# A state-space recurrence with its states in the partitions, sums by TensorE, and three smaller edits

## The chip, the cores and the metric

The kernel runs on one core of a Trainium2 chip. The metric is the device time of one execution in microseconds (us), as the median of several runs. One execution was also recorded by the hardware profiler; the line numbers (L1053) are those of the kernel before. PE is TensorE, DVE VectorE, ACT ScalarE, POOL GpSimd; SP issues DMAs.

## The reference

Six layers run one after the other over x of 64 sequences x 32 steps x 256 channels, each added to x: cross-attention to a context of 257 rows (stage 0), a time-mixing layer with a recurrence (1), a mixture of experts with the two best of eight (2), a quantized cross-attention (3), a state-space layer (4) and a mixture of eight experts (5). The change touches stages 0, 4 and 5. Cut to what matters, stage 0 is

```python
q = querys @ Wq.T + bq
k = keys @ Wk.T + bk
v = values @ Wv.T + bv
scores = jnp.einsum('bnd,bmd->bnm', q, k)
```

and stage 4, with 512 inner channels d and 16 states n, is

```python
ssm = xc @ x_proj_w.T + x_proj_b
B_param = ssm[..., :d_state]
C_param = ssm[..., d_state:2 * d_state]
delta = jax.nn.softplus(ssm[..., -1:])
A = -jnp.exp(A_log)
def step(h, ts):
    dt, B_t, C_t, x_t = ts
    dA = jnp.exp(A[None] * dt[:, :, None])
    dBx = dt[:, :, None] * B_t[:, None, :] * x_t[:, :, None]
    h = dA * h + dBx
    y = jnp.einsum('bdn,bn->bd', h, C_t) + D * x_t
    return (h, y)
```

followed by `y * silu(z)`, an output projection with a bias, the residual and a layer norm. Stage 5 begins with `logits = xf @ gate_w.T + gate_b`.

## The kernel before

The 2048 rows of x stay in SBUF as four blocks of 512 (16 sequences of 32 steps). The stages are written block by block in `layers`, in an order that lets one block's stage 4 run beside the next block's stage 3: `gates`, `ahead` of the next block, `recur`, stage 3 of the block after that, stage 5 of the block before. A scheduler takes each engine's instructions from that text and orders them, so that instructions of several stages alternate in each engine's queue; each queue is then worked through strictly in that order. Buffers come from pools with a fixed number of copies per tag, and whoever wants a copy waits until its last reader is done. Nearly all transfers of size are issued by SP, in one queue.

Stage 0. `head` (L173) normalizes a block, brings it to channels in partitions (`xnT`), makes q from it with Wq (L189, bias on ACT at L190), then `qk` from q with Wk (L196), so that scores are `qk` against the raw context (L241), with `qb` (L202) for the bias of the keys. `attend` ends with the value projection (L280) and its bias, a matmul of one row of ones against `bv` (L281).

Stage 4. `ahead` (L968) normalizes, projects (L965), convolves (L990), and makes `ssm` of 32 rows, B and C (L1000), which go to DRAM (`rows`, L1004). The step is made by a second product, with a weight column repeated 128 times, so that it stands in all partitions (`dt_ps`, L1008); a softplus of ACT and DVE instructions (L1013 to L1022) makes `dt`. All these PSUM tiles come from the pool `psp`, which has one buffer; so do those of `gates` (L1030), which makes `silu(z)`.

`recur` (L1032) has 128 of the 512 channels in the partitions and (sequence, step) along the free dimension. `dtx` = dt times the input is made by one POOL instruction (L1036). For each of 16 states, B's and C's rows are broadcast to all partitions (`bc`, L1045, 512 KB, two buffers); for each pair of channel groups POOL makes `g` = dtx times B (L1048), ACT makes the decay `h` = exp(A dt) into PSUM (L1052, two buffers), DVE runs the scan over it (L1053) and multiplies with C (`hc`, L1054), and POOL adds `hc` to `y` (L1055), which ACT had scaled with D (L1041). Then `y` is multiplied with the gate (L1058), projected (L1065), given its bias by a matmul of one row (L1066), added and normalized.

Stage 5. `block` makes gate logits with a bias by a matmul of one row (L1117), then 32 groups of up projections (L1160), gelu on ACT (L1164) and down projections (L1168), with PSUM tiles from `psu`, one buffer; w1 and w2 are loaded per expert by SP (L1155, L1156).

Of the kernel before, what the change touches and what calls it, by code (L numbers as in the profile page):

```python
# [135 lines left out]
def _stage0(k, pool):  # L136
# [11 lines left out]
    wq = _load_w(k, w, "L0_xattn_WqT", 2, D)  # L148
    wkk = _load_w(k, w, "L0_xattn_Wk", 2, D)
    wv = _load_w(k, w, "L0_xattn_WvT", 2, D)  # L150
    bv = w.tile([1, D], F32, name="bv", tag="bv")
    nc.scalar.dma_start(bv, i["L0_xattn_bv"])
# [3 lines left out]
    nc.vector.tensor_scalar(off, off, 0.0, None, ALU.is_equal)  # L156
    neg = w.tile([P, S], F32, name="neg", tag="neg")
# [15 lines left out]
    def head(b):  # L173
        x = k.x[b]
        xs = [x[:, j, :] for j in range(4)]
        mv, rstd = _stats(k, xs, "0", sm0)
        xn = blk.tile([P, 4, D], F32, name="xn", tag="xn")
        for j in range(4):
            _norm(k, xn[:, j, :], xs[j], mv, rstd, j)
        xnT = blk.tile([P, 2, BT], F32, name="xnT", tag="xT", bufs=3)  # L180
        _to_channels(
            k, [xn[:, j, :] for j in range(4)], lambda c, ps: nc.scalar.copy(xnT[:, c, :], ps),
            lambda shape, name: pa.tile(shape, F32, name=name, tag="a"),
        )
        qT = blk.tile([P, 2, BT], F32, name="qT", tag="xT", bufs=3)
        for o in range(2):
            ps = pa.tile([P, BT], F32, name="qps", tag="a")
            for c in range(2):
                nc.tensor.matmul(ps, wq[:, c, o * P : (o + 1) * P], xnT[:, c, :], start=c == 0, stop=c == 1)  # L189
            nc.scalar.activation(qT[:, o, :], ps, AF.Identity, bias=_chan(k, "L0_xattn_bq", o))  # L190

        qk = blk.tile([P, 2, BT], F32, name="qk", tag="xT", bufs=3)
        for d in range(2):
            ps = pa.tile([P, BT], F32, name="qkps", tag="a")
            for o in range(2):
                nc.tensor.matmul(ps, wkk[:, o, d * P : (d + 1) * P], qT[:, o, :], start=o == 0, stop=o == 1)  # L196
            nc.scalar.copy(qk[:, d, :], ps)
        qb = sm0.tile([P, 4], F32, name="qb", tag="qb")
        ps = pb.tile([P, 4], F32, name="qbps", tag="b")
        for j in range(4):  # L200
            for o in range(2):
                nc.tensor.matmul(  # L202
                    ps[:, j : j + 1], qT[:, o, j * P : (j + 1) * P], _chan(k, "L0_xattn_bk", o),
                    start=o == 0, stop=o == 1,
                )
        nc.scalar.copy(qb, ps)
        return qk, qb
# [28 lines left out]
    def attend(b, j, qk, qb, cT, cn, cl):  # L236
# [42 lines left out]
        for c in range(2):  # L279
            nc.tensor.matmul(o_ps, avT[:, c, :], wv[:, c, :], start=c == 0, stop=False)  # L280
        nc.tensor.matmul(o_ps, k.ones[0:1, :], bv, start=False, stop=True)  # L281
# [636 lines left out]
def _stage4(k, w, wk):  # L918
# [3 lines left out]

    nc, i = k.nc, k.i
# [4 lines left out]
    bx = w.tile([2 * N, 1], F32, name="bx", tag="bx")  # L928
    nc.scalar.dma_start(bx, i["L1_attn_x_proj_b"][0 : 2 * N, :])
    bdt = w.tile([P, 1], F32, name="bdt", tag="bdt")  # L930
    nc.scalar.dma_start(bdt, i["L1_attn_x_proj_b"][2 * N, :].partition_broadcast(P))
    rows = w.tile([40, D], F32, name="brows", tag="brows")
    bout, k.b2 = rows[0:1, :], rows[32:40, :]
    nc.scalar.dma_start(bout, i["L1_attn_out_proj_b"])
# [5 lines left out]
    A = w.tile([P, C, N], F32, name="A", tag="A")  # L940
    nc.scalar.dma_start(A, i["L1_attn_A_log"].rearrange("(c p) n -> p c n", p=P))
# [3 lines left out]

    wdt = w.tile([P, C, P], F32, name="wdt", tag="wdt")
    nc.vector.tensor_copy(wdt, wx[:, :, 2 * N : 2 * N + 1].to_broadcast([P, C, P]))
# [8 lines left out]
    def pp(shape, name):  # L956
        return k.psp.tile(shape, F32, name=name, tag="p")
# [10 lines left out]
    def ahead(b):  # L968
# [9 lines left out]
        _to_channels(k, xn, lambda c, ps: nc.scalar.copy(v.xT[:, c, :], ps), pp)  # L978

        xc = wk.tile([P, C, 16, T], F32, name="xc", tag="xc")  # L980
        for c in range(C):
            xpad = xpads[c % 2]
            nc.scalar.activation(
                xpad[:, :, 3:], project(v, c, pp).rearrange("p (b t) -> p b t", t=T), AF.Identity, bias=_chan(k, "L1_attn_in_proj_b", c)
# [11 lines left out]


        ssm_ps = pp([2 * N, BT], "ssm_ps")
        for c in range(C):
            nc.tensor.matmul(ssm_ps, wx[:, c, 0 : 2 * N], v.y[:, c, :], start=c == 0, stop=c == C - 1)  # L1000
        ssm = tmp([2 * N, BT], "ssm")
        nc.scalar.activation(ssm, ssm_ps, AF.Identity, bias=bx)
        v.rows = k.dram.tile([2 * N, BT], F32, name="rows", tag="rows", bufs=2)
        nc.sync.dma_start(v.rows, ssm)  # L1004

        dt_ps = pp([P, BT], "dt_ps")
        for c in range(C):
            nc.tensor.matmul(dt_ps, wdt[:, c, :], v.y[:, c, :], start=c == 0, stop=c == C - 1)  # L1008


        dt = v.dt = wk.tile([P, BT], F32, name="dt", tag="dt")
        e_, u_, l_ = (tmp([P, BT], n) for n in ("e_", "u_", "l_"))
        nc.scalar.activation(dt, dt_ps, AF.Identity, bias=bdt)  # L1013
        nc.scalar.activation(e_, dt_ps, AF.Abs, bias=bdt)
# [8 lines left out]

        return v

    def gates(v):

        v.zs = wk.tile([P, C, BT], F32, name="zs", tag="zs", bufs=1)
        for c in range(C):
            nc.scalar.activation(v.zs[:, c, :], project(v, C + c, pp), AF.Silu, bias=_chan(k, "L1_attn_in_proj_b", C + c))  # L1030

    def recur(b, v):  # L1032
        xs = [k.x[b][:, j, :] for j in range(4)]
        dt, y = v.dt, v.y
        dtx = wk.tile([P, C, BT], F32, name="dtx", tag="dtx", bufs=1)
        nc.gpsimd.tensor_tensor(dtx, y, dt.unsqueeze(1).to_broadcast([P, C, BT]), ALU.mult)  # L1036

        nc.gpsimd.memset(dt.rearrange("p (b t) -> p b t", t=T)[:, :, 0:1], 1e20)

        for c in range(C):  # L1040
            nc.scalar.activation(y[:, c, :], y[:, c, :], AF.Copy, scale=_chan(k, "L1_attn_D", c))  # L1041
        bc_rows = v.rows.rearrange("(two n) t -> n two t", two=2)
        for n in range(N):
            bc = wk.tile([P, 2, BT], F32, name="bc", tag="bc", bufs=2)
            nc.sync.dma_start(bc, bc_rows[n].partition_broadcast(P))  # L1045
            for c2 in range(0, C, 2):
                g = wk.tile([P, 2, BT], F32, name="g", tag="g", bufs=2)
                nc.gpsimd.tensor_tensor(g, dtx[:, c2 : c2 + 2], bc[:, 0:1, :].to_broadcast([P, 2, BT]), ALU.mult)  # L1048
                hc = wk.tile([P, 2, BT], F32, name="hc", tag="hc", bufs=2)
                for c in range(2):  # L1050
                    h = ph([P, BT], "h")
                    nc.scalar.activation(h, dt, AF.Exp, scale=A[:, c2 + c, n : n + 1])  # L1052
                    nc.vector.tensor_tensor_scan(h, h, g[:, c, :], 0.0, ALU.mult, ALU.add)  # L1053
                    nc.vector.tensor_tensor(hc[:, c, :], h, bc[:, 1, :], ALU.mult)  # L1054
                nc.gpsimd.tensor_tensor(y[:, c2 : c2 + 2], y[:, c2 : c2 + 2], hc, ALU.add)  # L1055

        for c2 in range(0, C, 2):
            nc.gpsimd.tensor_tensor(y[:, c2 : c2 + 2], y[:, c2 : c2 + 2], v.zs[:, c2 : c2 + 2], ALU.mult)  # L1058
        xn = wk.tile([P, 4, D], F32, name="xe4", tag="hc", bufs=2)
        xn = [xn[:, j, :] for j in range(4)]  # L1060
        for j in range(4):
            _norm(k, xn[j], xs[j], v.mv, v.rstd, j)
            ps = ph([P, D], "outps")
            for c in range(C):
                nc.tensor.matmul(ps, y[:, c, j * P : (j + 1) * P], wout[:, c, :], start=c == 0, stop=False)  # L1065
            nc.tensor.matmul(ps, k.ones[0:1, :], bout, start=False, stop=True)  # L1066
            nc.vector.tensor_tensor(xn[j], ps, xn[j], ALU.add)
# [13 lines left out]
def _stage5(k, w, out):  # L1081
# [5 lines left out]
    bg = w.tile([1, E], F32, name="bg", tag="bg")  # L1087
    nc.scalar.dma_start(bg, i["L1_ffn_gate_b"])
# [9 lines left out]
    for o in range(2):  # L1098
        nc.tensor.matmul(bs_ps[:, o : o + 1], k.b2[:, o * P : (o + 1) * P], k.ones[32 : 32 + E, 0:1], start=True, stop=True)
# [3 lines left out]
    def block(b):  # L1103
# [12 lines left out]
        for j in range(4):  # L1116
            nc.tensor.matmul(lg_ps[:, j, :], k.ones[0:1, :], bg, start=True, stop=False)  # L1117
            for c in range(2):
                nc.tensor.matmul(lg_ps[:, j, :], xT[:, c, j * P : (j + 1) * P], wg[:, c, :], start=False, stop=c == 1)  # L1119
# [9 lines left out]
        nc.vector.tensor_copy(lg, lg_ps)  # L1129
# [144 lines left out]
def _layouts(inputs):  # L1274
# [11 lines left out]
        "L0_xattn_WqT": a["L0_xattn_Wq"].T,  # L1286
        "L0_xattn_Wk": a["L0_xattn_Wk"],
        "L0_xattn_WvT": a["L0_xattn_Wv"].T,
        "L0_xattn_bv": a["L0_xattn_bv"][None, :],
# [7 lines left out]
    for n in ("L1_xattn_ln_gamma", "L1_xattn_ln_beta", "L1_attn_ln_gamma", "L1_attn_ln_beta", "L1_attn_A_log"):  # L1297
        o[n] = a[n]
    for n in ("in_proj", "x_proj", "out_proj"):
        o[f"L1_attn_{n}T"] = a[f"L1_attn_{n}_w"].T  # L1300
    o["L1_attn_x_proj_b"] = a["L1_attn_x_proj_b"][:, None]
    o["L1_attn_out_proj_b"] = a["L1_attn_out_proj_b"][None, :]
    o["L1_ffn_gate_wT"] = a["L1_ffn_gate_w"].T
    o["L1_ffn_gate_b"] = a["L1_ffn_gate_b"][None, :]
# [24 lines left out]
```

## Time and profile before

| | us |
|---|---|
| median of 3 runs (lowest, highest) | 2099.14 (2093.59, 2099.62) |
| the profiled execution | 2096.84 |
| its span, first to last instruction | 2095.1 |
| recurrence of block 0, 1, 2, 3 (windows from the span's start) | 776 to 1013, 1104 to 1326, 1443 to 1654, 1757 to 1913 |
| stage 5 of the last block | 1951 to 2095 |

The page divides the span into 40 equal slices; each digit is the busy share in tenths:

```profile
PE   4778966669979788656487798887888987787798
...
DVE  5587584775584559889767988655888755876100
ACT  3445342304434174444146566356557445664232
POOL 4445445312121325667625777513767634998000
```

One slice is 52 us. The recurrences lie in slices 16 to 37. A matmul's end is modelled, and passes overlap by their tails, so a busy PE is not a full one; a float32 matmul of the kernel is two passes in the trace. In the lines of groups, the columns are line, engine, operation, output and inputs, count, then busy us, mean ns of one, and after the second bar the engine's idle us just before such instructions, with what ended it.

### The profile page before, as it was taken

What the parts mean: (1) busy time and instruction counts of PE and PEld (TensorE: products, weight loads), DVE (VectorE), ACT (ScalarE), POOL (GpSimd) and SP (SyncE); (2) the same over time, 40 slices, a digit from 0 to 9 for tenths busy, and PEclk for the clock granted to TensorE, in tenths of its full rate; (3) what the DMA queues carried; (4) which work ended last, traced back from release to release, by engine and by line L of the source; (5) the groups of instructions that cost most, each with busy time, mean ns of one, the idle gap of its engine ahead of it and who ended that gap; (6) DMA issues with size and microseconds to landing.
All of it is one profiled execution on the core that took longest, in us unless ns stands there. A gap on an engine that the chain in (4) does not pass through costs nothing. (4 is left out here: it accounts for less than half of the span.)

```text
span 2095.1 us, 20245 instructions
## 1 busy us (share of the span) xinstructions
PE 1644.2 (78%) x6455; PEld 834.1 (40%) x6455; DVE 1391.0 (66%) x2444; ACT 952.6 (45%) x2009; POOL 1013.9 (48%) x1037
## 2 busy tenths in 40 slices
PE   4778966669979788656487798887888987787798
PEld 2334534335545434433234344433444433233343
DVE  5587584775584559889767988655888755876100
ACT  3445342304434174444146566356557445664232
POOL 4445445312121325667625777513767634998000
PEclk8677977889989898558687899888799887999799
DMA  7654232210001011121011232112232112332021
GB/s 239 219 182 144 91 120 80 79 34 21 21 21 43 17 42 51 30 61 61 0 50 53 80 91 90 31 41 65 71 88 73 49 31 66 89 111 77 30 81 40
DMA packets 87540, 149.93 MB, mean 72 GB/s; under 512 B 7672, under 2 KB 51978, under 8 KB 85386
## 3 DMA queue, kind: packets, MB, share of 16 engines
q1 hardware_dynamic: 84868, 147.69, 23.0%
q10 hardware_dynamic: 2566, 0.96, 0.2%
q8 instruction: 51, 0.84, 0.2%
q14 instruction: 55, 0.45, 0.1%
HBM read 137.71 MB, written 10.91 MB: 71 GB/s over the span
## 5 line engine op out<-in xcount | busy, mean ns | idle before, releaser
L1048 POOL TENSOR_TENSOR g<-dtx,bc 128x1024 f32<-128x1024 f32 x128 | 300.4, 2353 | 194.8 <-DVE h L1053 89.4
L1053 DVE TENSOR_TENSOR_SCAN h<-h,g 128x512 f32<-128x512 f32 x256 | 307.3, 1218 | 49.9 <-ACT h L1052 35.1
L1160 PE MATMUL up<-xT,w 128*128 128x512 f32 x512 | 288.1, 678 | 42.5 <-ACT hid L1162 37.3
L1055 POOL TENSOR_TENSOR xc<-xc,hc 128x1024 f32<-128x1024 f32 x128 | 301.0, 2356 | 26.5 <-DVE hc L1054 14.8
L1168 PE MATMUL acc<-hid,w 128*128 128x512 f32 x512 | 250.9, 610 | 15.8 <-ACT hid L1164 15.7
L1052 ACT ACTIVATE h<-dt,A 128x512 f32<-128x512 f32 x256 | 174.0, 692 | 184.5 <-DVE hc L1054 183.3
L1054 DVE TENSOR_TENSOR hc<-h,bc 128x512 f32<-128x512 f32 x256 | 169.7, 679 | 2.9 <-POOL xc L1055 0.5
L1160 PEld LDWEIGHTS up<-xT,w 128*128 128x128 f32 x512 | 97.3, 209 | 165.3 <-issue 79.2
L839 ACT ACTIVATE p<-sc,nm 128x256 f32<-128x256 f32 x256 | 117.6, 471 | 94.5 <-DVE nm L835 83.2
L1162 ACT ACTIVATE hid<-up,chan 128x512 f32<-128x512 f32 x128 | 87.2, 681 | 159.5 <-PE up L1160 159.4
L614 PE MATMUL weps<-we,xT 128*128 128x512 f32 x256 | 139.3, 665 | 17.2 <-DVE x L616 13.9
L1168 PEld LDWEIGHTS acc<-hid,w 128*128 128x128 f32 x512 | 94.1, 194 | 128.2 <-issue 96.3
L828 PE MATMUL sc<-kT,qm 32*128 32x256 f32 x512 | 131.6, 448 | 14.9 <-DVE od L867 11.5
L852 PE MATMUL pt_ps<-ident,p 128*128 128x128 f32 x512 | 97.0, 328 | 53.7 <-ACT p L839 26.6
L833 DVE TENSOR_REDUCE nm<-sc 128x2 f32<-128x512 f32 x128 | 86.3, 686 | 56.2 <-PE sc L828 55.1
L89 POOL TENSOR_TENSOR rs_t<-rs_r 128x4 f32<-128x4 f32 (+3 forms) x138 | 29.7, 218 | 183.1 <-DVE rs_r L87 157.0
L852 PEld LDWEIGHTS pt_ps<-ident,p 128*128 128x128 f32 x512 | 69.5, 165 | 107.1 <-ACT p L839 64.4
L828 PEld LDWEIGHTS sc<-kT,qm 32*128 32x128 f32 x512 | 81.5, 208 | 70.5 <-DVE od L867 20.7
L230 POOL TENSOR_TENSOR cT<-cT,scb 128x2056 f32<-128x2056 f32 x16 | 74.5, 4657 | 53.5 <-DMA scb<-scales 51.8
L1181 DVE SCALAR_TENSOR_TENSOR o<-rT,gt,x 128x256 f32<-128x256 f32 x16 | 7.7, 483 | 139.4 <-PE rT L1180 132.5
L854 ACT COPY pt<-pt_ps 128x512 f32<-128x512 f32 x128 | 74.0, 588 | 40.5 <-PE pt_ps L852 40.3
L514 POOL TENSOR_TENSOR kk<-kk 128x512 f32<-128x512 f32 x32 | 33.1, 1040 | 103.8 <-ACT kk L513 103.8
(389 smaller groups left out, 3218.7 us busy)
## 6 DMA issues: line engine op xcount, KB each, us to landing
bc<-rows SPq DMA_DIRECT2D x64, 512.0 KB
w<-in_L_ffn_w_dram SPq DMA_DIRECT2D x64, 512.0 KB
cT<-in_ctxT_dram SPq DMA_DIRECT2D x16, 1028.0 KB
cq<-cq SPq DMA_DIRECT2D x32, 514.0 KB
cn<-in_ctx_dram SPq DMA_DIRECT2D x64, 256.0 KB
scb<-scales SPq DMA_DIRECT2D x16, 514.0 KB
kb<-steps SPq DMA_DIRECT2D x16, 514.0 KB
x<-in_x_dram SPq DMA_DIRECT2D x4, 512.0 KB
```

The costliest lines, as they stand in the source:

```text
L614: nc.tensor.matmul(ps, xT[:, c, r], we[:, c, e : e + 2, :], start=c == 0, stop=c == 1)
L828: nc.tensor.matmul(sc[h][:, f, :], qm[r, e + f].rearrange("p l n g -> p (l n g)"), kTs[e][r, f, :], start=True, stop=True,)
L839: nc.scalar.activation(w_[:, f, h - h0, :], sc[h][:, f, :], AF.Exp, bias=nm[:, e + f, h : h + 1], accum_out=sm[:, e + f, h : h + 1],)
L852: nc.tensor.transpose(pt_ps[:, h, m, :], ws[e0, hp][:, f, h, m * P : (m + 1) * P], k.ident)
L1048: nc.gpsimd.tensor_tensor(g, dtx[:, c2 : c2 + 2], bc[:, 0:1, :].to_broadcast([P, 2, BT]), ALU.mult)
L1052: nc.scalar.activation(h, dt, AF.Exp, scale=A[:, c2 + c, n : n + 1])
L1053: nc.vector.tensor_tensor_scan(h, h, g[:, c, :], 0.0, ALU.mult, ALU.add)
L1054: nc.vector.tensor_tensor(hc[:, c, :], h, bc[:, 1, :], ALU.mult)
L1055: nc.gpsimd.tensor_tensor(y[:, c2 : c2 + 2], y[:, c2 : c2 + 2], hc, ALU.add)
L1160: nc.tensor.matmul(u, w1[e][:, c, q * P : (q + 1) * P], xT[:, c, :], start=c == 0, stop=c == 1)
L1162: nc.scalar.activation(hid[e][:, q, :], u, AF.Identity, bias=b1)
L1168: nc.tensor.matmul(acc[o], w2[e][:, q, o * P : (o + 1) * P], hid[e][:, q, :], start=n == H, stop=n == E * H + H - 1)
```

## The change

Stage 4. The partitions now hold 16 states x 8 channels. B and C are brought into that layout once per block (`bc`, state n in partitions 8n to 8n+7) instead of once per state. `dtx` is made in `ahead` by four POOL instructions and written to DRAM; for each group of 8 channels SP fetches their eight rows broadcast over the 16 states. The product with B, the exponential, the scan and the product with C have the shapes and counts they had; `y` is no longer added on POOL. Instead TensorE sums over the 16 states with a matrix of ones and zeros (`red`): each group of 8 channels lands in its rows of a PSUM tile `y_ps`, 16 groups to a tile, and DVE adds D times the input as it reads the tile. `total` is called one pair of groups late. The step is row 33 of `ssm` and comes back from DRAM broadcast to all partitions. PSUM tiles of `ahead` come from stage 3's pool `ps` (two buffers), those of `gates` from `psu`, and `psp` is left to `y_ps`.

Biases. `bv` is added to x by POOL in `head`, the output projection's bias by POOL in `recur`, the gate's bias by DVE as it reads the logits; the three matmuls of one row go. Stage 0. The product of Wq and Wk is made once on TensorE, with the products of the biases, and `qk` comes from `xnT` by one projection instead of two.

```diff
 # stage 0
+    for c in range(2):
+        r = slice(c * P, (c + 1) * P)
+        ps = pa.tile([P, D + 4], F32, name="wqk_ps", tag="a")
+        for o in range(2):
+            nc.tensor.matmul(ps[:, 0:D], wq[:, o, r], wkk[:, o, :], start=o == 0, stop=o == 1)
...
-        for o in range(2):
-            ps = pa.tile([P, BT], F32, name="qps", tag="a")
-            for c in range(2):
-                nc.tensor.matmul(ps, wq[:, c, o * P : (o + 1) * P], xnT[:, c, :], start=c == 0, stop=c == 1)
-            nc.scalar.activation(qT[:, o, :], ps, AF.Identity, bias=_chan(k, "L0_xattn_bq", o))
+        for j in range(4):
+            nc.gpsimd.tensor_tensor(xs[j], xs[j], bv, ALU.add)
...
-        nc.tensor.matmul(o_ps, k.ones[0:1, :], bv, start=False, stop=True)
 # stage 4, ahead
-        dt_ps = pp([P, BT], "dt_ps")
-        for c in range(C):
-            nc.tensor.matmul(dt_ps, wdt[:, c, :], v.y[:, c, :], start=c == 0, stop=c == C - 1)
+        rows = k.dram.tile([M, BT], F32, name="rows", tag="rows", bufs=2)
+        nc.sync.dma_start(rows, ssm)
         dt = v.dt = wk.tile([P, BT], F32, name="dt", tag="dt")
+        nc.sync.dma_start(dt, rows[2 * N].partition_broadcast(P))
+        v.bc = wk.tile([P, 2, BT], F32, name="bc", tag="bc")
+        for j in range(2):
+            nc.sync.dma_start(v.bc[:, j], rows[j * N : (j + 1) * N].unsqueeze(1).to_broadcast([N, 8, BT]))
...
+        for c in range(C):
+            dtx = tmp([P, BT], "dtx")
+            nc.gpsimd.tensor_tensor(dtx, v.y[:, c], dt, ALU.mult)
+            nc.sync.dma_start(v.dtx[2 * c : 2 * c + 2].rearrange("h p t -> (h p) t"), dtx)
 # stage 4, recur
-        for c in range(C):
-            nc.scalar.activation(y[:, c, :], y[:, c, :], AF.Copy, scale=_chan(k, "L1_attn_D", c))
...
+        def total(c, q, h2, hc, ps):
+            for r in range(2):
+                m = 32 * (2 * h2 + r)
+                nc.tensor.matmul(
+                    ps[m : m + 32, :], red[:, 24 - 8 * q : 56 - 8 * q], hc[:, r, :], start=q == 0, stop=q == 3, skip_group_check=True,
+                )
+            if q == 3 and h2 == 1:
+                nc.vector.scalar_tensor_tensor(y[:, c, :], y[:, c, :], _chan(k, "L1_attn_D", c), ps, ALU.mult, ALU.add)
+                nc.gpsimd.tensor_tensor(y[:, c, :], y[:, c, :], v.zs[:, c, :], ALU.mult)
...
+            ps = k.psp.tile([P, BT], F32, name="y_ps", tag="p")
+            for n in range(8):
+                q, h2 = divmod(n, 2)
+                g = wk.tile([P, 2, BT], F32, name="g", tag="g", bufs=3)
+                for r in range(2):
+                    nc.sync.dma_start(g[:, r], dtx[2 * c + h2, q, r].unsqueeze(0).to_broadcast([N, 8, BT]))
+                nc.gpsimd.tensor_tensor(g, g, v.bc[:, 0:1, :].to_broadcast([P, 2, BT]), ALU.mult)
+                hc = wk.tile([P, 2, BT], F32, name="hc", tag="hc", bufs=3)
+                for r in range(2):
                     h = ph([P, BT], "h")
-                    nc.scalar.activation(h, dt, AF.Exp, scale=A[:, c2 + c, n : n + 1])
-                    nc.vector.tensor_tensor_scan(h, h, g[:, c, :], 0.0, ALU.mult, ALU.add)
-                    nc.vector.tensor_tensor(hc[:, c, :], h, bc[:, 1, :], ALU.mult)
-                nc.gpsimd.tensor_tensor(y[:, c2 : c2 + 2], y[:, c2 : c2 + 2], hc, ALU.add)
+                    at = c * G + 4 * (2 * h2 + r) + q
+                    nc.scalar.activation(h, dt, AF.Exp, scale=A[:, at : at + 1])
+                    nc.vector.tensor_tensor_scan(h, h, g[:, r, :], 0.0, ALU.mult, ALU.add)
+                    nc.vector.tensor_tensor(hc[:, r, :], h, v.bc[:, 1, :], ALU.mult)
+                late.append((c, q, h2, hc, ps))
+                if len(late) > 1:
+                    total(*late.pop(0))
...
-            nc.tensor.matmul(ps, k.ones[0:1, :], bout, start=False, stop=True)
 # stage 5
-            nc.tensor.matmul(lg_ps[:, j, :], k.ones[0:1, :], bg, start=True, stop=False)
...
-        nc.vector.tensor_copy(lg, lg_ps)
+        nc.vector.tensor_tensor(lg, lg_ps, bg.unsqueeze(1).to_broadcast([P, 4, E]), ALU.add)
```

## What was predicted

> **What bounds the kernel now.** First the busy shares of the page, then the costliest groups, then busy time in eleven stretches that I cut where a recurrence begins or ends, then who the vector engine waited for.
>
> ```profile
> PE 1644.2 (78%) x6455; PEld 834.1 (40%) x6455; DVE 1391.0 (66%) x2444; ACT 952.6 (45%) x2009; POOL 1013.9 (48%) x1037
> ...
> L1048 POOL TENSOR_TENSOR g<-dtx,bc 128x1024 f32<-128x1024 f32 x128 | 300.4, 2353 | 194.8 <-DVE h L1053 89.4
> L1053 DVE TENSOR_TENSOR_SCAN h<-h,g 128x512 f32<-128x512 f32 x256 | 307.3, 1218 | 49.9 <-ACT h L1052 35.1
> ...
> L1055 POOL TENSOR_TENSOR xc<-xc,hc 128x1024 f32<-128x1024 f32 x128 | 301.0, 2356 | 26.5 <-DVE hc L1054 14.8
> ...
> L1054 DVE TENSOR_TENSOR hc<-h,bc 128x512 f32<-128x512 f32 x256 | 169.7, 679 | 2.9 <-POOL xc L1055 0.5
> ```
>
> No engine is full over the whole span, so the stages decide. (Window, its length, then PE, PE loads, DVE, ACT, POOL busy, TensorE clock, DMA share, GB/s.)
>
> ```profile
> 0.00:440.00 440.00, 305.75 (x1305) 162.01 (x1305) 296.31 (x507) 174.15 (x493) 198.77 (x277) 0.77 0.44 141
> ...
> 776.00:1013.00 237.00, 158.82 (x772) 88.48 (x770) 206.99 (x327) 100.52 (x252) 150.20 (x90) 0.68 0.16 45
> ...
> 1104.00:1326.00 222.00, 183.36 (x804) 92.80 (x808) 185.00 (x260) 138.61 (x279) 155.00 (x92) 0.85 0.27 80
> ...
> 1443.00:1654.00 211.00, 175.58 (x772) 88.08 (x770) 179.84 (x259) 134.30 (x273) 151.11 (x78) 0.87 0.25 72
> ...
> 1757.00:1913.00 156.00, 115.76 (x257) 47.54 (x256) 122.90 (x145) 95.12 (x120) 145.98 (x75) 0.94 0.32 91
> ```
>
> The last four rows are the recurrences of blocks 0 to 3. In the first three, which share the core with stage 3 of the next block, DVE is 87, 83 and 85% busy and PE 67, 83 and 83%: DVE leads, PE is close behind it, POOL is not the bound. Only the fourth is bound by POOL (146 of 156 us): a pair of groups costs it 2.35 + 2.36 = 4.7 us, and DVE 2 x 1.22 + 2 x 0.68 = 3.8. After it comes stage 5 of the last block, 144 us of almost pure PE.
>
> Who DVE waited for in the second recurrence, and what POOL does to it without a wait:
>
> ```profile
> DVE h L1053 <- ACT h L1052: 10.3, 9, 3.5
> DVE kT L809 <- PE kT_ps L807: 9.6, 3, 4.7
> DVE st L101 <- POOL o L907: 6.6, 3, 2.8
> DVE nm L833 <- PE sc L828: 4.6, 4, 3.5
> ```
> ```profile
> 1213.90 2.35 POOL L1055 TENSOR_TENSOR xc<-xc,hc 128x1024 f32<-128x1024 f32 x1
> 1214.15 2.12 DVE L835 TENSOR_TENSOR nm<-nm,nsl 128x4 f32<-128x4 f32 x1
> ```
>
> Four elements per partition took 2.12 us; the same line's median is 0.164. It began just after POOL's addition and ended with it (1216.25).
>
> **POOL's additions (L1055) go.** 128 x 2.356 = 301 us of POOL. In the first three recurrences little DVE waiting is POOL's: summed over all its gaps, DVE idled there for PE 19, 18 and 15 us, for ACT 5, 10 and 9, for POOL 4, 7 and 7. The larger thing hides in durations. If for each DVE form I add up the time above its fastest tenth, the three stretches hold 32 + 31 + 25 = 88 us. Here the Trainium skill and the row part: GPSIMD Engine Reference, Key points, says that POOL contends with vector instructions that have two SBUF inputs or use both ports. Read as shared bandwidth (at most a halving), L835's 64 instructions would lose 64 x 0.16 = 10 us; the row shows a stop until POOL is done, and they lost 26. I follow the row. The scan and hc read h from PSUM and keep 1.22 and 0.68 whatever POOL does. The additions are 71 of some 150 POOL us in each stretch, so 0.45 x 88 = **-40 us**, and half of POOL's own 18 us of DVE waits, -9.
>
> **Sums on TensorE come.** 128 groups, each two matmuls of 128x32 by 512 columns, two passes each. The pitch of a 512-column pass is 0.43 us at full clock (eight passes of L1168 in a run take 3.60). L862, also 32 columns wide, starts passes for different 32-row strips of PSUM 6 to 7 ns apart, so the two matmuls of a group overlap: 2 x 0.43 = 0.86 us, 27.5 us a block, 110 in all; not overlapped it is 220. Against the change speaks TensorEngine Tiling, Key Properties: switching the tiling mode drains the array. It names no price; the trace has one: from L1168 to L862 522 ns where 429 is the pitch, 0.09 a switch, two a group, +24 us: 134 instead of 110. PE loses: q projection 32 passes x 0.43 = 14; dt_ps 32 x 0.43 = 14; bias passes L281 and L1066, 32 each at 0.32 = 20. Net about **+86 us of PE**, nearly all of it inside the recurrences: +33 each, at clocks of 0.68 to 0.87 some 40. That takes PE to about 84% in the first and above 95% by busy time in the next two (busy overstates: passes overlap by their tails). DVE waited 52 us for PE in these stretches; behind a waiting sum stand stage 3's scores (L828), and behind those DVE's nm (L833). Bounds: 0 (stage 5's matmuls give way, they are not urgent) to +60. I take **+20**, nearer to nothing because the sums run one group late and because stage 5 can slip. Each block also gains four DVE reads of y_ps: 12 x 0.75 (L990's form) = **+9**; the four ACT scalings (L1041) go, off the path.
> First three recurrences: -40 - 9 + 20 + 9 = **-20** (bounds -70 to +60).
>
> **Fourth recurrence.** POOL falls to 2.35 us a pair, DVE leads with 3.8 + 0.2 (the hand-over hc, exp, scan, 1841.75 to 1842.59 beside the second hc) = 4.0, x 32 = 128, plus 3 for y. Gelu and its two table loads (4.5 us on ACT, L1164) come 7 or 8 times and hold the next exps back by about 2 us each: +16. 147 for 156; PE needs 116 + 33 there and is then as full as DVE. **-8** (bounds -22 to +10).
>
> **The g stream.** Before: 64 broadcasts of 512 KB. Now 256 of 256 KB, +33 MB, dtx 4 MB, against 150 MB at 23% of the engines: +6 points of DMA time, hidden. The loop through three buffers: two issues 0.8 + landing 5.0 (bc, chain of waits: 4.95 to 6.65) + POOL 2.35 + two scans 2.44 = 10.6 per three pairs, 3.5 a pair. It is faster than DVE's 4.0, but by little. 0 (bounds 0 to +50).
>
> **The way into each recurrence (ahead).** dt_ps (3.6 us in the trace) becomes: ssm 0.7, a write of the rows 1.8 (issue 1730.40 to the next at 1732.17), a broadcast of 256 KB about 3 (between out's 2.1 and bc's 5.0): +1.9. dtx, one POOL instruction of 4.51, becomes four of 1.1, a write 2.1, a read of g 4, then the product 2.35: 9.6 for 6.9, +2.7. Two PSUM buffers for the projections instead of one give back about 2. +2.6 x 4 = **+10** (bounds 0 to +30); it counts because the stretches between the recurrences are chains in which DVE is half idle.
>
> **Stage 0.** Besides the 14 + 10 us of PE: eight ACT evictions (L190, 0.69) fewer, and one stage of PE-ACT less before each block's scores (qps began 24.90, qkps 29.28: 4.4 us). Added: 16 passes of 256 columns for the product of the weights at half clock, 7 us, before block 0's scores only; 16 POOL additions of bv, 0.72 each. PE has 306 of 440 us and DVE 296: neither is the bound all along. **-10** (bounds -25 to +8). **Tail**: one bias pass group, 1.2, and the gate's bias, 0.7: **-2**.
>
> **Sum**: -20 - 8 + 10 - 10 - 2 = -30 us on the profiled execution's 2096.8 (span 2095.1): **2067 us**. The median of the runs, 2099.1, lies 2.3 higher, within their spread.
>
> **Rivals.** *PE becomes the bound* (slower). Place: the second and third recurrence. PE is in order, so a sum that waits for hc stops stage 3's and stage 5's matmuls. For it: PE already 83% there, DVE's largest waits are on PE. Against it: a clock of 0.85 and tails leave real room, and stage 5 is movable. If two thirds of the net 86 us / 0.85 = 101 stay on the path (+67), with ahead +10 and -40 from POOL: 2134. It decides from PE shares near 95%. *SP blocks g* (slower): w loads (L1155) waited 289 us on SP for PE, up to 48.8, and g stands behind such loads. Against it: bc stood there too and POOL waited for it only 21 us. 30 loads among g at 3 us: +90, less 20: 2167. *DVE runs full* (much faster): if all waits for POOL go and the extra matmuls raise the clock (0.68 in the first recurrence), DVE's 572 us in three stretches become 521 at 92%: 566 for 670, and with 20 each from stage 0 and the fourth: 1953. *It does not do what it says*: the instruction order shows the sums, 64 matmuls a block, spread through each recurrence, so no.
>
> **How the numbers follow.** My forecast has 0.44, DVE full 0.16, PE bound 0.27, SP blocking 0.13. The forecast's own range is 2030 to 2100. The range 1985 to 2150 takes in part of every rival. A measurement tells 0.3% (6 us) from no change: faster 0.16 + 0.36 = 0.52; same 0.08; slower 0.40.
>
> **What would show it.** L835 and L115 near their medians in the first three recurrences: the port part is right. DVE waits on PE there above 90 us in place of 52: PE is the bound. Waits of POOL's product for g's landing above 60 us: SP or the g stream. The fourth recurrence at 140 to 150 us with POOL below 60%. Wrong altogether if DVE in the first three recurrences stays below 80% busy.

## The result and the profile after

| | before | after |
|---|---|---|
| median of the runs (lowest, highest), us | 2099.38 (2093.59, 2105.84) | 2123.32 (2116.53, 2130.91) |
| the profiled execution, its span | 2096.84, 2095.1 | 2130.91, 2129.1 |
| start of the first to start of the last scan, blocks 0, 1, 2, 3 | 228.0, 212.5, 204.2, 155.7 | 222.7, 213.0, 231.7, 180.1 |
| start to first scan | 785.6 | 778.2 |
| from one recurrence's last scan to the next one's first | 93.9, 124.9, 104.5 | 94.9, 113.0, 111.4 |
| last scan to the end | 185.8 | 184.1 |

The ratio after to before is 1.0113, 95% interval 1.0074 to 1.0152: slower, where 2067 was forecast. The lower rows add up to the 34 us between the two spans: +47 in the recurrences, of which the third and fourth have all, -7 before them, -4 between them, -2 at the end. The forecast had -28 in the recurrences.

First the busy shares and the costliest groups of the page of after (L1083 is the old L1048, L1089 and L1090 the old L1053 and L1054; the old L1055 is gone, L1068 is new).

```profile
PE 1766.4 (83%) x6835; PEld 812.3 (38%) x6835; DVE 1338.8 (63%) x2460; ACT 931.1 (44%) x1981; POOL 759.9 (36%) x962
...
L1083 POOL TENSOR_TENSOR g<-g,bc 128x1024 f32<-128x1024 f32 x128 | 300.5, 2350 | 437.6 <-DMA g<-dtx 385.5
L1089 DVE TENSOR_TENSOR_SCAN h<-h,g 128x512 f32<-128x512 f32 x256 | 307.4, 1220 | 109.4 <-ACT h L1088 80.8
L1068 PE MATMUL y_ps<-hc,red 128*32 128x512 f32 x512 | 265.4, 658 | 36.8 <-DVE hc L1090 36.2
...
L1198 ACT ACTIVATE hid<-up,chan 128x512 f32<-128x512 f32 x128 | 87.5, 684 | 237.7 <-PE up L1196 237.6
```

POOL lost its additions and DVE 52 us of busy time, as meant. But the sums, 256 matmuls of two passes each, keep TensorE busy for 265 us; the forecast had put 134. (As in the prediction, a group is the two sums made from one `hc`; each writes its own strip, 32 of the 128 rows of `y_ps`.) The windows of the four recurrences (columns as in the prediction):

```profile
770.00:1001.00 231.00, 190.74 (x910) 81.50 (x909) 193.31 (x330) 94.55 (x247) 84.87 (x53) 0.87 0.32 93
...
1090.00:1309.00 219.00, 210.71 (x866) 85.78 (x865) 163.97 (x253) 125.22 (x257) 83.21 (x50) 0.95 0.42 121
...
1418.00:1654.00 236.00, 217.32 (x880) 87.58 (x878) 167.39 (x254) 134.67 (x271) 83.90 (x51) 0.94 0.35 105
...
1765.00:1945.00 180.00, 168.10 (x349) 48.01 (x350) 120.63 (x148) 91.73 (x116) 79.58 (x48) 0.94 0.40 117
```

PE is 83, 96, 92 and 93% busy, DVE 84, 75, 71 and 67%. From the second on they have changed places, although the granted clock has risen (0.68 to 0.87 in the first, 0.85 to 0.95 in the second). POOL, which bound the fourth, is 44% busy there. The chain that ended last, by engine:

```profile
PE 56%; DVE 18%; POOL 9%; ACT 6%; issue 6%; DMA 4%; SPq 0%; ACTq 0%; DVEq 0%; POOLq 0%
```

Why the sums cost twice what they should is seen in the timeline of the fourth recurrence (start, duration, engine, line, what, how many passes):

```profile
1851.07 1.04 PE L1068 MATMUL y_ps<-hc,red 128*32 128x512 f32 x2
...
1852.05 1.13 PE L1204 MATMUL acc<-hid,w 128*128 128x512 f32 x2
...
1853.10 1.05 PE L1068 MATMUL y_ps<-hc,red 128*32 128x512 f32 x2
...
1854.08 1.12 PE L1196 MATMUL up<-xT,w 128*128 128x512 f32 x2
...
1857.28 0.69 ACT L1198 ACTIVATE hid<-up,chan 128x512 f32<-128x512 f32 x1 [4.22 <-PE up L1196]
```

Each sum stands alone: one strip's matmul, then one of stage 5, then the other strip's. In the whole trace 176 sums stand alone, and only 25 times do the two of a group follow each other. From the start of a lone sum to the start of the stage 5 matmul right behind it are 0.976 us (median of 116), so nothing overlaps, and the matmul ahead of it takes 523 ns to the next start where 429 is the pitch, the usual time from one pass's start to the next. A group's two `hc` are done at different times, 3.6 us apart in the median, so there is room for another matmul between the two sums; that the scheduler filled it for this reason is supported by e1 below.

The last line above shows how this reaches DVE. Its waits in the second recurrence (who for whom: us in total, times, longest), and then the waits of all engines in the fourth:

```profile
DVE nm L849 <- PE sc L844: 18.7, 11, 5.2
DVE h L1089 <- ACT h L1088: 12.4, 6, 5.2
```
```profile
ACT hid L1198 <- PE up L1196: 62.9, 21, 9.1
DVE h L1089 <- ACT h L1088: 43.1, 26, 7.2
...
DVE h L1089 <- POOL g L1083: 11.4, 1, 11.4
```

In the second, stage 3's scores (L844) stand behind the sums, and `nm` behind them: it waited 18.7 us, where before had 4.6. In the fourth it is indirect: the scan waits 43 us "for ACT", but ACT had stood in its own queue at stage 5's `hid` (L1198), which waited 63 us for TensorE, with the next exponential behind it.

### The profile page after: what moved, and what is told of

Same layout as the page of the kernel before. It is cut to its first block, busy times and chain, and to the rows that moved or that the text cites. A ratio compares the mean times of both kernels' runs of the same rounds, so it can differ in the third digit from the quotient of the medians.

```text
span 2129.1 us, 21332 instructions
## 1 busy us (share of the span) xinstructions
PE 1766.4 (83%) x6835; PEld 812.3 (38%) x6835; DVE 1338.8 (63%) x2460; ACT 931.1 (44%) x1981; POOL 759.9 (36%) x962
## 4 chain that ended last, share of the span: by engine, by line
PE 56%; DVE 18%; POOL 9%; ACT 6%; issue 6%; DMA 4%; SPq 0%; ACTq 0%; DVEq 0%; POOLq 0%
PE acc L1204 9%; PE up L1196 9%; PE y_ps L1068 8%; PE sc L844 3%; PE weps L630 3%; DVE h L1089 3%; PE pt_ps L868 2%; PE cv L539 2%; PE oT_ps L878 2%; PE ck L527 2%; DMA g<-dtx 2%; DVE nm L849 1%; DVE hc L1090 1%; PE outps L1103 1%; POOL g L1083 1%
## 5 line engine op out<-in xcount | busy, mean ns | idle before, releaser
L1083 POOL TENSOR_TENSOR g<-g,bc 128x1024 f32<-128x1024 f32 x128 | 300.5, 2350 | 437.6 <-DMA g<-dtx 385.5
L1089 DVE TENSOR_TENSOR_SCAN h<-h,g 128x512 f32<-128x512 f32 x256 | 307.4, 1220 | 109.4 <-ACT h L1088 80.8
L1068 PE MATMUL y_ps<-hc,red 128*32 128x512 f32 x512 | 265.4, 658 | 36.8 <-DVE hc L1090 36.2
L1196 PE MATMUL up<-xT,w 128*128 128x512 f32 x512 | 276.4, 643 | 20.2 <-ACT hid L1198 19.9
L1198 ACT ACTIVATE hid<-up,chan 128x512 f32<-128x512 f32 x128 | 87.5, 684 | 237.7 <-PE up L1196 237.6
L1090 DVE TENSOR_TENSOR hc<-h,bc 128x512 f32<-128x512 f32 x256 | 169.6, 680 | 1.5 <-PE y_ps L1068 0.3
L855 ACT ACTIVATE p<-sc,nm 128x256 f32<-128x256 f32 x256 | 117.5, 471 | 104.5 <-DVE nm L851 104.2
L1196 PEld LDWEIGHTS up<-xT,w 128*128 128x128 f32 x512 | 90.0, 197 | 172.4 <-issue 126.5
L630 PE MATMUL weps<-we,xT 128*128 128x512 f32 x256 | 132.8, 641 | 9.1 <-DVE x L632 5.8
L844 PE MATMUL sc<-kT,qm 32*128 32x256 f32 x512 | 123.3, 416 | 8.0 <-DVE od L883 5.4
L868 PE MATMUL pt_ps<-ident,p 128*128 128x128 f32 x512 | 85.8, 297 | 22.2 <-ACT p L855 18.8
L844 PEld LDWEIGHTS sc<-kT,qm 32*128 32x128 f32 x512 | 77.3, 192 | 60.1 <-issue 11.2
L89 POOL TENSOR_TENSOR rs_t<-rs_r 128x4 f32<-128x4 f32 (+3 forms) x138 | 34.6, 254 | 182.9 <-DVE rs_r L87 174.8
L868 PEld LDWEIGHTS pt_ps<-ident,p 128*128 128x128 f32 x512 | 61.8, 150 | 79.0 <-ACT p L855 36.4
L1068 PEld LDWEIGHTS y_ps<-hc,red 128*32 128x32 f32 x512 | 34.8, 112 | 146.9 <-DVE hc L1090 79.9
```

The lines of the kernel that those rows point to most:

```text
L630: nc.tensor.matmul(ps, xT[:, c, r], we[:, c, e : e + 2, :], start=c == 0, stop=c == 1)
L844: nc.tensor.matmul(sc[h][:, f, :], qm[r, e + f].rearrange("p l n g -> p (l n g)"), kTs[e][r, f, :], start=True, stop=True,)
L855: nc.scalar.activation(w_[:, f, h - h0, :], sc[h][:, f, :], AF.Exp, bias=nm[:, e + f, h : h + 1], accum_out=sm[:, e + f, h : h + 1],)
L868: nc.tensor.transpose(pt_ps[:, h, m, :], ws[e0, hp][:, f, h, m * P : (m + 1) * P], k.ident)
L1068: nc.tensor.matmul(ps[m : m + 32, :], red[:, 24 - 8 * q : 56 - 8 * q], hc[:, r, :], start=q == 0, stop=q == 3, skip_group_check=True,)
L1083: nc.gpsimd.tensor_tensor(g, g, v.bc[:, 0:1, :].to_broadcast([P, 2, BT]), ALU.mult)
```

## The experiments

Theory A: the strips stand apart, so the sums fill TensorE, and TensorE is the bound. Theory B: SP's 256 loads of g are the bound (POOL waited 385 us for them). Theory C: the moved PSUM buffers are. Busy times are of the profiled execution, in us; the clock is the mean granted TensorE clock over its span. The runs come from more than one chip, and each ratio is to runs of the kernel before made with them.

| kernel | sums busy | PE busy | clock | median us | ratio to before (95%) |
|---|---|---|---|---|---|
| after | 265.4 | 1766 | 0.881 | 2123 | 1.0113 (1.0074 to 1.0152) |
| e6_four_plain | 267.0 | 1771 | 0.876 | 2128 | 1.0141 (1.0116 to 1.0166) |
| e11_wide | 290.3 | 1757 | 0.890 | 2113 | 1.0095 (1.0069 to 1.0122) |
| e1_reversed | 152.0 | 1680 | 0.868 | 2082 | 0.9922 (0.9873 to 0.9972) |
| e3_quarter | 68.5 | 1628 | 0.859 | 2046 | 0.9744 (0.9694 to 0.9793) |
| e2_four | 77.0 | 1604 | 0.868 | 2028 | 0.9668 (0.9621 to 0.9715) |
| e10_xe4_g | 75.2 | 1602 | 0.871 | 2014 | 0.9617 (0.9573 to 0.9660) |
| e9_bf16 | 32.3 | 1613 | 0.842 | 2047 | 0.9758 (0.9735 to 0.9781) |
| e7_dt_pe | 84.5 | 1670 | 0.846 | 2069 | 0.9884 (0.9832 to 0.9937) |
| e8_four_gpsq | 85.4 | 1644 | 0.857 | 2084 | 0.9940 (0.9922 to 0.9958) |
| e4_no_add | none | 1637 | 0.843 | 2039 | 0.9714 (0.9672 to 0.9756) |
| e5_stage0 | none | 1634 | 0.835 | 2099 | 1.0015 (1.0001 to 1.0028) |

**e1_reversed**: only the order of a group's two strips.

```diff
-            for r in range(2):
+            for r in (1, 0):
```

> The changed kernel, with the two matmuls of a group written in the other order (r = 1 before r = 0), so that both are ready when the first is and they stand side by side in TensorE's order (118 pairs of 128; in the changed kernel 25). Theory A (strips apart: alone, a sum costs 1.04 us and the pair does not overlap, so the sums fill TensorE with 265 us where 134 were forecast): busy time of the sums near 130, the third and fourth recurrences back to about 205 and 150 us, 2050 to 2075 us in all. Theory B (SP and the g stream hold the recurrence back): 2115 to 2130, sums cheaper but nothing gained. Theory C (the PSUM tiles of ahead and gates moved into the pools of stages 3 and 5 hold these up): 2110 to 2130.

2082: the strip whose `hc` comes last goes first, so both are ready together, and in the trace 110 pairs now follow each other. Here is a pair, four passes, and what comes behind it:

```profile
1785.64 1.05 PE L1068 MATMUL y_ps<-hc,red 128*32 128x512 f32 x4 [0.48 <-DVE hc L1090]
1786.63 3.70 PE L1204 MATMUL acc<-hid,w 128*128 128x512 f32 x8
```

A pair takes 0.983 us from its start to the next matmul's (median), a lone sum 0.976. One edit of order took 113 us off the sums and 41 off the time; the range was missed by 7. The loads of g and the moved buffers are as in after, so B and C, which expected no gain, fall.

**e2_four**: the four strips of two groups together (the delay by one group goes too).

```diff
-        def total(c, q, h2, hc, ps):
-            for r in range(2):
-                m = 32 * (2 * h2 + r)
+        def total(c, q, hcs, ps):
+            for m4 in (3, 2, 1, 0):
+                m = 32 * m4
...
-                late.append((c, q, h2, hc, ps))
-                if len(late) > 1:
-                    total(*late.pop(0))
-        total(*late.pop(0))
+                late.append(hc)
+                if h2 == 1:
+                    total(c, q, late, ps)
+                    late = []
```

> The changed kernel, with the sums of two groups made together, four strips side by side (63 fours in TensorE's order). Theory A: sums near 64 x 1.05 = 67 us of TensorE, 2030 to 2060 us, at or below the kernel with pairs. Theories B and C: 2110 to 2130.

2028, faster than both kernels. In its timeline of TensorE one such four, eight passes, and what comes behind it:

```profile
1796.59 1.06 PE L1068 MATMUL y_ps<-hc,red 128*32 128x512 f32 x8 [1.17 <-DVE hc L1090]
1797.59 1.13 PE L1196 MATMUL up<-xT,w 128*128 128x512 f32 x2
1798.55 3.60 PE L1204 MATMUL acc<-hid,w 128*128 128x512 f32 x8
```

Four sums take 0.995 us (median), nearly as long as one. The recurrences fell to 211.6, 199.1, 197.2 and 140.3.

**e3_quarter**: three quarters of the sums are left out, so y lacks the sums of 96 of every 128 channels (those that stay set both `start` and `stop`).

```diff
-            for r in range(2):
+            for r in range(2) if q == 3 else ():
...
```

> The changed kernel with only the last quarter of the sums (q = 3); the other three quarters of y's sum over the channels of a tile are left out. Theory A: sums near 66 us of TensorE though still apart, so about the time of the four strips together, 2030 to 2060 us. Theories B and C: 2110 to 2130, since g, the buffers and the pools stay as they are.

2046, with sums of 68.5 us: no faster than e2, which makes all of them in 77.0. So it is TensorE's time that counts here, and not how many sums there are.

**e6_four_plain**: e2 with its strips in ascending order.

```diff
-            for m4 in (3, 2, 1, 0):
+            for m4 in range(4):
```

> As e2, the sums of two groups called together once every second group, but with the four strips in ascending order, so that in TensorE's order most of them (191 of 256) again stand alone between other stages' matmuls. Theory A (what costs is that strips stand apart, each with its own two passes and two switches): the sums are busy 200 us or more, TensorE above 1700 us, and the time is near the changed kernel's, 2085 to 2135. Rival (what helped e2 is that the sums are called half as often, or only another order): 2020 to 2060, with the sums' busy time still above 200 us.

2128: as slow as after. Calling the sums half as often is worth nothing; the strips stand apart again, 181 alone, and all that e2 won is gone.

**e11_wide**: after, with no strips: every sum adds into all 128 partitions.

```diff
-                    ps[m : m + 32, :], red[:, 24 - 8 * q : 56 - 8 * q], hc[:, r, :], start=q == 0, stop=q == 3, skip_group_check=True,
+                    ps, red[:, 120 - 8 * q - m : 248 - 8 * q - m], hc[:, r, :], start=q + h2 + r == 0, stop=q == 3 and h2 + r == 2,
```

> The changed kernel, in its own order of sums, but each sum is a 128x128 matmul (ones in the 8 columns that belong to its group, zeros in the others) that adds into all 128 partitions: no strips, so no overlap and no change of tiling either. Theory A splits the 265 us of sums into passes and switches: 256 x 2 x 0.43 = 220 us stay and 256 x 2 x 0.09 = 46 us of switches go. PE then falls from 1766 to about 1720, and as PE sets the pace the time falls by 20 to 45: 2080 to 2105. If the price was in the strips themselves (the switch costs more than 0.09, or the lone strip's passes run longer), sums below 210 and the time below 2075; if the switches cost nothing, 2110 or more.

2113, and its interval covers most of after's, so no gain is shown; the sums are busy 290 us and not the 220 expected. The switches went only between matmuls of stage 5: there a lone sum takes 0.859 us to the next matmul (median of 13), and the matmul ahead of it 429 ns, not 523. Stage 3's matmuls are tiled otherwise (L844 32x128, L878 128x32), and from a sum to one of these it still takes 522 ns; the sums' weight loads, now 128 columns wide, take 0.20 us and not 0.11. So e11 does not price the switches. After's own trace does, beside stage 5: 0.09 ahead of a lone sum and 0.12 in it, 0.21 of 1.07 us, the smaller part.

What e11 does show is how the work moves: the four recurrences are 72 us shorter than after's (207.0, 193.5, 206.6 and 168.4), but after the last scan 245 us follow where after had 184. Stage 5 had been put off, and TensorE has to do it then:

```profile
1696.00:1865.00 169.00, 145.35 (x333) 59.41 (x332) 126.41 (x153) 92.37 (x114) 79.06 (x47) 0.96 0.44 125
1865.00:1985.00 120.00, 105.36 (x264) 50.95 (x264) 18.16 (x51) 30.29 (x33) 19.20 (x51) 0.92 0.20 62
```

In the second row DVE is 15% busy and TensorE 88%.

**e4_no_add**: the kernel before, with POOL's additions left out for 15 of 16 states, so y lacks those states.

```diff
-                nc.gpsimd.tensor_tensor(y[:, c2 : c2 + 2], y[:, c2 : c2 + 2], hc, ALU.add)
+                if n == N - 1:
+                    nc.gpsimd.tensor_tensor(y[:, c2 : c2 + 2], y[:, c2 : c2 + 2], hc, ALU.add)
```

> The kernel before, with POOL's addition to y left out for 15 of the 16 states: what the additions cost where they stood, with nothing put in their place. If POOL's instructions stop the vector engine as forecast (40 us of longer vector instructions and 9 of waits in the first three recurrences, and some 10 in the fourth): 2030 to 2050 us. If those long instructions lie beside other waits and cost nothing: only the fourth recurrence gains, 2080 to 2092 us.

2039, as expected: the additions cost about 58 us. The recurrences are 207.2, 193.0, 195.6 and 148.7, that is 49 less in the first three and 7 less in the fourth.

**e8_four_gpsq**: e2, with the second half of each g issued by POOL.

```diff
-                    nc.sync.dma_start(g[:, r], ...)
+                    (nc.sync if r == 0 else nc.gpsimd).dma_start(g[:, r], ...)
```

> As e2, but the second half of each g comes from POOL's own queue and not from SP's, so SP issues 128 broadcasts and not 256, as before the change. Theory A: the g stream bounds nothing, so no gain: 2020 to 2050, the upper end if POOL's products wait behind their own issues. Rival (SP's queue holds g behind weight loads, 385 us of POOL waits for g): a gain of 20 us or more, below 2010, and those waits fall to half.

2084, some 57 us over e2 by the ratios (0.027 of 2096), worse than either theory expected. Taking half of the loads off SP gained nothing, which speaks against B once more, though it put a new load on POOL: 128 issues of 0.54 us. The waits in the fourth recurrence of this kernel:

```profile
POOL g L1083 <- DMA g<-dtx: 65.3, 23, 4.5
DVE h L1089 <- POOL g L1083: 41.1, 21, 4.3
```

In e2 the two are 36.5 and 18.6. An issue now stands in POOL's order behind products that wait for earlier loads; that this is the cause is likely but not shown. Of the 52 us between the two profiled spans, 18 lie in the fourth recurrence and 28 between the recurrences.

**e9_bf16, e10_xe4_g, e7_dt_pe**: e2 with bf16 sums (one pass); e2 with the buffer alone that e9 also had to move; e2 with dt made by TensorE again (its bias by ACT).

```diff
 # e9
-                hc = wk.tile([P, 2, BT], F32, name="hc", tag="hc", bufs=3)
+                hc = wk.tile([P, 2, BT], BF16, name="hc", tag="hc", bufs=3)
...
 # e9 and e10
-        xn = wk.tile([P, 4, D], F32, name="xe4", tag="hc", bufs=3)
+        xn = wk.tile([P, 4, D], F32, name="xe4", tag="g", bufs=3)
 # e7
-        nc.sync.dma_start(dt, rows[2 * N].partition_broadcast(P))
+        dt_ps = pa([P, BT], "dt_ps")
+        for c in range(C):
+            nc.tensor.matmul(dt_ps, wx[:, c, 2 * N : 2 * N + 1].to_broadcast([P, P]), v.y[:, c, :], start=c == 0, stop=c == C - 1)
...
```

> As e2, but hc and the matrix of ones are bf16, so that each sum is one pass and not two; hc loses its low 16 bits, which changes y by rounding. If TensorE's time still sets the pace in e2's recurrences (77 us of sums), halving them gives 2000 to 2022. If in e2 the bound has gone back to the vector engine's scan, hc and the way between recurrences, nothing: 2022 to 2035, unless DVE's hc changes its own duration from 0.68 us, which then shows in the group's mean.

> e2 with the one buffer moved that the bf16 kernel moved too (xe4 takes g's buffers and not hc's), sums in f32. If the bf16 kernel's 2047 came from that buffer: 2040 to 2055. If it came from its one-pass sums (a lower granted clock, 0.84 against 0.87, with fewer passes on TensorE): as e2, 2020 to 2035, at a clock near 0.87.

> e2 with the row through DRAM undone: dt comes from four matmuls with the step's column broadcast, as before the change (+14 us of TensorE, between the recurrences). The prediction priced the row's way at +1.9 us a block, so this one should be 0 to 10 us faster than e2: 2015 to 2030. If the row's way is hidden by bc's, which goes the same way: 2025 to 2040.

None of the three came as expected: e10 lies 6 us below its lowest range, e9 12 and e7 29 above their highest. The buffer is not at fault: e10 gives 2014, the lowest time here (its interval and e2's overlap). e9 halved the sums, with `hc` still 0.68 us on DVE, and is slower; e7 was to add 14 us to TensorE, and PE's busy time rose by 66. Both have a lower clock. The second recurrence of e10, e9 and e7:

```profile
1092.00:1289.00 197.00, 179.38 (x897) 82.50 (x895) 168.00 (x240) 130.87 (x262) 81.33 (x42) 0.98 0.43 129
```
```profile
1095.00:1295.00 200.00, 176.79 (x797) 85.47 (x798) 164.11 (x252) 124.73 (x255) 86.62 (x57) 0.88 0.44 124
```
```profile
1100.00:1295.00 195.00, 174.52 (x823) 84.07 (x822) 163.18 (x245) 117.42 (x243) 80.24 (x48) 0.88 0.44 123
```

In about the same time e10 gets 897 passes done, e9 797, e7 823; what is not done is left for later. In both, the scheduler's order differs from e2's, and stage 5 of block 0 begins late: at 1112 and 1117 us, after the recurrence's first scan (1095 and 1100), in e2 and e10 at 1079 and 1075, before it (1094 and 1092). Whether the order, the clock or the clock through the order is the cause was not separated. So neither run prices its edit, and a difference of some 40 us between two such kernels is not a cause by itself; that of 100 us between e2 and e6 goes with 190 us of sums and lies well beyond it.

**e5_stage0**: the kernel before with the edits of stage 0 alone (the product of the weights, one projection, `bv` on POOL), as in the diff above.

> The kernel before with only stage 0's edits: the two query projections made one and bv added by POOL. Forecast of the prediction: -10, so 2085 to 2093. The changed kernel's trace has the first scan 7 us earlier: 2090. If the gain is lost on the way to the first scan or in later stages: 2095 to 2105.

2099, 1.0015 (1.0001 to 1.0028): no gain. TensorE's busy time in the first 500 us did fall, from 359 to 342, but it was not what the stage waited for: the scores began at 34.8, 93.3, 170.8 and 275.0 us in the four blocks before, now at 40.2, 98.3, 165.8 and 280.2. The first comes later, behind the product of the weights; of the others only the third is earlier, and the first scan came 7 us later (792.9 against 785.6). The clock between 400 and 500 us fell too, 0.83 to 0.74.

## Why the prediction was wrong, by its steps

The forecast had -30 us and the span grew by 34. Of these 64 us, 43 lie in the first three recurrences (forecast -20, measured +23) and 32 in the fourth (-8, and +24, outside its bounds of -22 to +10); the ways between came out 14 below the forecast, the start 3 above.

**The step that failed**: "L862, also 32 columns wide, starts passes for different 32-row strips of PSUM 6 to 7 ns apart, so the two matmuls of a group overlap: 2 x 0.43 = 0.86 us, 27.5 us a block, 110 in all". The rate was right, but that the two would be neighbours was not looked at: L862's matmuls stand next to each other in TensorE's order, the sums do not. Lone, each costs its own two passes and its own two switches: 265 us in place of 134. Beside it stood "not overlapped it is 220", which was dropped without a look at the order. The instruction order of the changed kernel has the lone sums in it; the prediction read from it only that they are spread. e1, e2 and e6 show the cause both ways: with the strips adjacent 2028, the same kernel with them apart 2128.

**The switch's price** was sized right. The Trainium skill, TensorEngine Tiling (Array Packing), Key Properties, says that changing the tiling mode drains the array; in after this is 0.09 us ahead of a sum, as forecast, and 0.12 in the sum itself (0.976 for two passes of 0.429). But a lone sum pays both, where the forecast had two switches for a group.

**Fourth recurrence -8**: failed by the same step. With "PE needs 116 + 33 there" the sums would have fitted; a quarter of 265 is 66, and 116 + 66 = 182 is what the recurrence took (180, with PE busy 168). With four strips together it took 140, with POOL 55% busy there (77 of 141 us), as the forecast wanted.

**"DVE waits for PE +20, bounds 0 to +60"**: the waits that end with PE did rise by 20 in the first three recurrences, from 52 to 72 us. What had no term is the way through ACT: DVE's waits for ACT rose from 24 to 62, with ACT waiting for TensorE ahead of the exponential. So the sign "above 90" on PE was too narrow. "Waits of POOL's product for g's landing above 60" was no good sign either: there were 385 us, and the scan waited for POOL's `g` 27 us in all (POOL was 36% busy). The sign "Wrong altogether if DVE in the first three recurrences stays below 80% busy" came in two of three (84, 75 and 71%).

**Right**: the additions, -40 in durations and -9 in waits. e4's first three recurrences are 49 shorter, and the excess of DVE's durations there, added up for each operation and shape over its fastest tenth, is 91 in before (the prediction had 88), 47 in e4 and 49 in after. **Tail -2**: -2.

**Other terms**: **ahead +10** was -4 between the recurrences in after, +12 in e2. **g stream 0** was not measured alone; e2, with all loads of g on SP, is no slower than e4, which only drops the additions, so it is unlikely to have cost much. **Stage 0 -10**: wrong, 0 to +6 by e5; the step took a shorter chain on TensorE and ACT for a shorter stage. In after the first scan still came 7 us earlier: there the input projection, with two PSUM buffers, took 23 us (726.9 to 749.7) and not 52.

**The rival that came**: PE as the bound, 2134 worked out, 2123 measured. Its point, "PE shares near 95%", was met. That its number came so near is luck: it put 86 us more on PE, and PE's busy time rose by 122. Its place was met in part: the second recurrence (96%) kept its length, the third got longer, and so did the fourth, which it did not name. e11 shows why the place is hard to tell: what TensorE does not do in one stretch it owes in the next.

## What to carry to other kernels

Here matmuls into different strips of PSUM shared their time only where they stood next to each other in TensorE's order; with a scheduler between text and queue, make them ready together (the one whose input comes last goes first) and read the order that results. When an engine near 85% takes on work, add up its whole span: the loss may show in a later stage, and reach the other engines through queues in which something else waits for it.

## What was not expected of the hardware

One, two and four sums that stand together take 0.976, 0.983 and 0.995 us to the next matmul: three of four cost 0.02 us together. A DVE instruction of 0.16 us still took up to 2.33 beside POOL's remaining products (L851; median 0.157). It began 0.04 us after such a product and ended with it. And the granted clock does not tell which kernel is faster: with the sums apart it was higher than before (0.881 against 0.836 over the span) and the time longer; with one-pass sums (e9) it was 0.842, with 32 passes more (e7) 0.846, against 0.871 in e10, and both were slower. Why was not found out.
